# Experts with 33 to 96 tokens past their first 128: three groups behind the tile, groups by column halves, branches ahead of the last tile

## The chip, the cores and the metric

The kernel runs on one core of one Trainium2 chip. The metric is the device time of one execution in microseconds (us). All arithmetic is fp32. The engines are named as in the profile: PE is TensorE (PEld its weight loads), DVE VectorE, ACT ScalarE, POOL GpSimd, SP SyncE; a trailing q means an engine's instruction sequencer (branches, waits on semaphores, issue of DMAs).

## What is computed

A perceiver layer on 512 tokens (8 x 64) of width 512: cross-attention to a context of 1601 rows, a causal linear-attention block with its MLP, and a mixture of experts. Only the last part is touched by the change:

```
logits = x @ w_router                       # 8 experts
top 2 experts per token, softmax over the two logits -> gating
for each expert e:
    hmid = silu(x @ w0[e]) * (x @ w1[e])    # width 1024
    out += gating[:, e] * (hmid @ wo[e])
```

Each expert is needed only for the tokens that chose it. With the inputs of the reference the eight experts have 133, 104, 217, 159, 87, 132, 70 and 122 tokens (counted by running the reference's router). So experts 0, 3 and 5 have 5, 31 and 4 tokens past their first 128, and expert 2 has 89.

## The kernel before, in words

The first stages end at about 424 us. From there the experts run one after the other; everything below is about them.

Order. The program order of every engine is the order of the source (a manual schedule), so what stands behind a wait on an engine waits too. Weights come through a ring of 12 buffers of 1 MB: `need` (L201) frees buffers whose work is past and issues the loads up to 7 places ahead on SP, which in practice loads expert e+1 while expert e is computed. An expert has four `e_up` parts (256 columns of w0 beside 256 of w1, 512 in all) and two `e_wo` parts.

Places. A rank per token and expert gives a table with the tokens of each expert in tiles of 128 (`tabulate`, L924; `late_places`, L1161). `fetch` (L1030) gathers the rows of a tile by an indirect DMA on POOL; `turn_tile` (L1045) transposes them on PE. Tile (e, 0) is the first 128 tokens of expert e; key (e, 1) is the tokens that follow. Unused places point to spare rows.

A whole tile (`whole_tile`, L1088) is, for four quarters of the hidden width: `up` (4 matmuls of 512 columns), silu on ACT and product on DVE (`gated`, L1058), two transposes (`hidden_t`, L1065), and two matmuls into the sum `y`. `add_rows` (L1073) scales by the gate on ACT and adds to the output by an indirect scatter on POOL; each scatter waits for the one before it. Hooks `between(0..2)` put other work into a tile, such as the transposes of the next one.

A group (`group`, L1127) serves up to 32 tokens past the first 128. PE is split into four sets of 32 columns; the four quarters of the hidden width run side by side, one on each: 16 up matmuls of 512 columns, one `gated`, two transposes, 8 down matmuls, a copy of the partial sums (`parts`) and one matmul with `fold` that adds the four. Each step waits for the step before.

Control. The counts are on the chip only. `few` (L1172) is 1 for an expert with 129 to 160 tokens; each engine loads it into registers and branches at the end of each expert (L1326). An `If` that isn't taken runs a short false path instead: each engine waits until its own work so far is done, and adds to its semaphore what the body would have added; POOL runs an INC_SWDGE_SEM there.

Tokens beyond (an expert with over 160, and any third or fourth tile) are handled behind the last expert: `list_big` (L1187) lists such tiles in the order of experts, `big_tile` (L1272) loads the expert's six weight parts again, transposes, and runs `whole_tile`. `all_big` (L1329) nests seven such tiles, each inside the branch of the one before. Here expert 2's 89 tokens are the only such tile.

Of the kernel before, what the change touches and what calls it, by code (L numbers as in the profile page):

```python
# [15 lines left out]
F32 = mybir.dt.float32  # L16
# [17 lines left out]
NQ = 4  # L34
FQ = FE // NQ
R = P // NQ
NI = B * S // P
COLS = 4 * KC + FF // P + KC * NE
HELD = 8
# [7 lines left out]
def perceiver_kernel(  # L47
# [960 lines left out]
    if True:  # L1008


        def side_bank(side, name):
            return pse.tile([P, 512], F32, tag=f"mm{side}", bufs=3 - side, name=name)
# [32 lines left out]
        def turn_tile(key, n=P):  # L1045

            xg = fetched[key]
            name = f"xgt_{key[0]}_{key[1]}"
            bank = (y_bank("w", name) if n == P else side_bank(1, name))
            for c in range(KC):  # L1050
                nc.tensor.transpose(  # L1051
                    bank[:, c * n : (c + 1) * n], xg[:n, c * P : (c + 1) * P], ident[:n, :n]
                )
            xg_t = moe2.tile([P, KC, n], F32, tag=f"xgT{n}", name=f"xgT_{key[0]}_{key[1]}")
            evacuate(xg_t.rearrange("p c q -> p (c q)"), bank[:, : KC * n])
            turned[key] = xg_t

        def gated(side, bank, name):  # L1058
            act = moe2.tile([P, FQ], F32, tag=f"act{side}", name=f"act_{name}")
            nc.scalar.activation(act, bank[:, :FQ], AF.Silu)  # L1060
            hid = moe2.tile([P, FQ], F32, tag=f"mid{side}", name=f"mid_{name}")
            nc.vector.tensor_tensor(hid, bank[:, FQ:], act, ALU.mult)  # L1062
            return hid
# [63 lines left out]
        def group(e, up_of, down_of):  # L1127


            nm = f"{e}_1"  # L1130
            xg_t = turned[e, 1]
            bank = side_bank(1, f"up_{nm}")
            for c in range(KC):
                for q in range(NQ):
                    nc.tensor.matmul(  # L1135
                        bank[q * R : (q + 1) * R, :],
                        xg_t[:, c, :],
                        up_of[q][:, c, :],
                        start=(c == 0),
                        stop=(c == KC - 1),  # L1140
                    )
            h_t = hidden_t(1, gated(1, bank, nm), nm)
            bank = side_bank(1, f"yq_{nm}")
            for j in range(2):
                for q in range(NQ):
                    nc.tensor.matmul(
                        bank[q * R : (q + 1) * R, :],
                        h_t[:, j, q * R : (q + 1) * R],
                        down_of[q // 2][:, 2 * (q % 2) + j, :],
                        start=(j == 0),  # L1150
                        stop=(j == 1),
                    )
            parts = moe2.tile([P, D], F32, tag="parts", bufs=1, name=f"parts_{nm}")
            evacuate(parts, bank)
            y = y_bank(1, f"y_{nm}")
            nc.tensor.matmul(y[:R, :], fold, parts, start=True, stop=True)
            add_rows((e, 1), y, R, 1)

        if True:

# [5 lines left out]
                        slots[e, i] = (src[:, k : k + 1], dst[:, k : k + 1])  # L1166


            few = moe.tile([P, NE], F32, name="few")
            more = moe.tile([P, NE, NI - 1], F32, name="more")  # L1170
            nc.vector.tensor_scalar(more[:, :, 0], count, float(P + R), None, ALU.is_gt)
            nc.vector.scalar_tensor_tensor(few, count, float(P), more[:, :, 0], ALU.is_gt, ALU.subtract)  # L1172
            few_i = moe.tile([1, NE], mybir.dt.int32, name="few_i")
            nc.vector.tensor_copy(few_i, few[0:1, :])
            counted = "sums of comparisons of the experts' counts of tokens"

            def load_few():
                _, values = nc.values_load_multi_w_load_instructions(
                    few_i, min_val=0, max_val=1, skip_runtime_bounds_check_because=counted
                )  # L1180
                return values

            nmore = NE * (NI - 1)
            flat = "p e i -> p (e i)"
            control = moe.tile([1, 1 + 2 * NBIG], mybir.dt.int32, name="control")

            def list_big(k):  # L1187

                if k == 0:
# [9 lines left out]
                        sums, step = new, 2 * step  # L1199
                    listed["sums"] = sums  # L1200
                    nc.vector.tensor_copy(control[:, 0:1], sums[0:1, nmore - 1 :])
                else:
                    by_big = [P, NBIG, nmore]
                    picked = moe.tile(by_big, F32, name="picked")
# [10 lines left out]
                    for v, values in enumerate([number, which_e]):  # L1215
# [4 lines left out]
                        nc.vector.tensor_reduce(  # L1220
                            numbers[:, v * NBIG : (v + 1) * NBIG], found, AX.X, ALU.add
                        )
                    nc.vector.tensor_copy(control[:, 1:], numbers[0:1, :])
                    listed["big_e"] = numbers[:, NBIG:]

            def load_big():
                sp = (mybir.EngineType.SP,)
                _, (big,) = nc.values_load_multi_w_load_instructions(
                    control[:, 0:1], min_val=0, max_val=NBIG, skip_runtime_bounds_check_because=counted
                )  # L1230
                _, spots = nc.values_load_multi_w_load_instructions(
                    control[:, 1 : 1 + NBIG],
                    engines=sp,
                    min_val=0,
                    max_val=NE * NI - 1,
                    skip_runtime_bounds_check_because=counted,
                )
                _, experts = nc.values_load_multi_w_load_instructions(
                    control[:, 1 + NBIG :],
                    engines=sp,  # L1240
                    min_val=0,
                    max_val=NE - 1,
                    skip_runtime_bounds_check_because=counted,
                )
                return big, spots, experts

            listed = {}

# [9 lines left out]
            def gate_big(j):  # L1258
# [10 lines left out]
                )  # L1269
                slots["big", j] += (gate,)  # L1270

            def big_tile(j):  # L1272

                key = ("big", j)
                tiles = {}
                e = bass.ds(listed["experts"][j], 1)
                for q in range(NQ):
                    tiles["up", q] = ring.tile([P, 4, 512], F32, tag="ring", name=f"big_up_{j}_{q}")
                    nc.sync.dma_start(tiles["up", q], e_up[e, q].rearrange("o p c n -> p (o c) n"))
                    if q % 2:  # L1280
                        n = q // 2
                        tiles["wo", n] = ring.tile([P, 4, 512], F32, tag="ring", name=f"big_wo_{j}_{n}")
                        nc.sync.dma_start(
                            tiles["wo", n],
                            e_wo[e, n].rearrange("o p c n -> p (o c) n"),
                        )

                if j > 0:
                    fetch_big(j, read_big(j))
                turn_tile(key)  # L1290
                gate_big(j)
                whole_tile(
                    key,
                    [tiles["up", q] for q in range(NQ)],
                    [tiles["wo", n] for n in range(2)],
                )

            turned[0, 0] = xg_t0
            for e in range(NE):

                def between(k, e=e):
                    if e == 0 and k == 0:
                        late_places()
                        for key in [(1, 0), (0, 1), (0, 0), (1, 1), (2, 0), (2, 1)]:
                            fetch(key, R if key[1] else P)
                    if k == (2 if e == 0 else 1) and e + 1 < NE:
                        turn_tile((e + 1, 0))
                    if k == 2:
                        turn_tile((e, 1), R)
                    if e == 1 and k < 2:  # L1310
                        list_big(k)

                up_of = [need("e_up", e, q) for q in range(NQ)]
                down_of = [need("e_wo", e, n) for n in range(2)]
                whole_tile((e, 0), up_of, down_of, between)
                if e == 0:
                    few_of = load_few()
                if 3 <= e + 2 < NE:
                    for i in range(2):
                        fetch((e + 2, i), R if i else P)  # L1320
                if e == 3:
                    listed["big"], listed["spots"], listed["experts"] = load_big()
                    listed["pairs"] = read_big(0)
                if e == NE - 3:
                    fetch_big(0, listed["pairs"])
                with tc.If(few_of[e] > 0):  # L1326
                    group(e, up_of, down_of)

            def all_big(j):  # L1329
                with tc.If(listed["big"] > j):  # L1330
                    big_tile(j)
                    if j + 1 < NBIG:
                        all_big(j + 1)

            all_big(0)


_INS = [
# [89 lines left out]
```

## Time and profile before

| | us |
|---|---|
| three runs | 673.49, 671.36, 673.45 |
| median | 673.45 |
| the profiled execution | 672.11 |
| its span (first to last instruction) | 670.4 |
| first matmul of expert 0 | at 423.95 |
| tile of expert 1, first up to next tile's first up | 457.39 to 480.43 |
| last matmul of expert 7's tile, ends | at 635.65 |
| last matmul of the tile at the end, ends | at 659.04 |

The span and the profiled time differ by 1.7 us, which lies around the instructions. In the profile a row of a timeline has the start, the length, the engine, the source line, the tiles written and read with their shapes, the number of records, and in brackets how long the engine was idle before and what ended that. A fp32 matmul leaves two MATMUL records on PE and two LDWEIGHTS records on PEld. A row of a table by stretch has the stretch, its length, and for each engine the busy time and number of records, then the granted PE clock (1.00 is full), the DMA share and GB/s. A row by line has the number of records and minimum, median and maximum in ns, then the first and last start in us.

### The profile page before, as it was taken

How to read it: one execution, taken by the hardware profiler on the slowest of the kernel's cores; microseconds unless marked ns; L12 is line 12 of the kernel's file. 1: busy time of each engine (PE TensorE's matmuls, PEld its weight loads, DVE VectorE, ACT ScalarE, POOL GpSimd, SP SyncE). 2: the span in 40 equal slices, each digit the busy share in tenths (PEclk: the TensorE clock that was granted, in tenths of full speed). 3: DMA queues.
4: the chain of work that ended last, by engine and by line, in shares of the span. 5: the costliest groups of instructions: out<-in, count | busy, mean ns of one | idle time of the engine just before them, and what ended most of it. 6: DMA issues, size and time to landing. Idle time of an engine off the chain costs nothing. (4 is left out here: it accounts for less than half of the span.)

```text
span 670.4 us, 6808 instructions
## 1 busy us (share of the span) xinstructions
PE 627.2 (94%) x2664; PEld 291.2 (43%) x2664; DVE 175.5 (26%) x419; ACT 128.3 (19%) x240; POOL 61.6 (9%) x81
## 2 busy tenths in 40 slices
PE   4998989799999999999999998899999899999993
PEld 3743434243444444454444455433444344334441
DVE  4011323122316888650000045311210111100100
ACT  2241222220132223031011211211111211111110
POOL 2000000000000000060000001340202202210000
PEclk9998999899999999999999999799999999999997
DMA  8999999999421203030213115029389576694611
GB/s 326 420 420 389 420 384 418 374 386 413 194 111 43 85 1 127 1 126 18 107 64 125 63 64 188 3 69 350 137 314 337 176 314 229 205 359 177 269 16 19
DMA packets 24224, 138.08 MB, mean 206 GB/s; under 512 B 4164, under 2 KB 4164, under 8 KB 11896
## 3 DMA queue, kind: packets, MB, share of 16 engines
q1 hardware_dynamic: 20056, 129.90, 49.7%
q0 software_dynamic: 3024, 6.58, 4.4%
q10 hardware_dynamic: 1104, 1.07, 0.5%
q8 instruction: 25, 0.41, 0.2%
q14 instruction: 15, 0.12, 0.1%
HBM read 132.56 MB, written 4.97 MB: 205 GB/s over the span
## 5 line engine op out<-in xcount | busy, mean ns | idle before, releaser
L1097 PE MATMUL up<-e_up,xgT 128*128 128x512 f32 x224 | 100.2, 595 | 1.2 <-PEq L1326 1.2
L1097 PEld LDWEIGHTS up<-e_up,xgT 128*128 128x128 f32 x224 | 40.9, 190 | 50.4 <-issue 50.4
L1105 PE MATMUL y<-e_wo,hidT 128*128 128x512 f32 x128 | 61.0, 599 | 0.0
L808 PE MATMUL mlp<-w,hid_sb 128*128 128x512 f32 x128 | 58.8, 597 | 0.0
L1062 DVE TENSOR_TENSOR mid<-up,act 128x256 f32<-128x256 f32 x35 | 14.9, 425 | 162.4 <-ACT act L1060 162.4
L472 PE MATMUL av<-ctx,eT 128*64 128x512 f32 x192 | 50.2, 636 | 7.3 <-DMA ctx<-in_ctx_dram 6.5
L787 PE MATMUL hid<-v_sb,w 128*128 128x512 f32 (+2 forms) x144 | 56.6, 545 | 0.0
L423 PE MATMUL sc<-ctxT,pw_t 128*64 128x401 f32 (+1 forms) x256 | 48.1, 501 | 0.6 <-DMA ctxT<-in_ctx_T_dram 0.6
L787 PEld LDWEIGHTS hid<-v_sb,w 128*128 128x128 f32 x144 | 26.2, 190 | 29.1 <-issue 27.3
L808 PEld LDWEIGHTS mlp<-w,hid_sb 128*128 128x128 f32 x128 | 23.4, 190 | 24.9 <-issue 24.9
L1060 ACT ACTIVATE act<-up 128x256 f32<-128x256 f32 x35 | 13.4, 384 | 104.5 <-PE up L1097 95.6
L1078 POOL DMA_INDIRECT out_dram<-y_sb,dst_late x11 | 16.8, 1530 | 160.9 <-ACTq L1326 103.7
L423 PEld LDWEIGHTS sc<-ctxT,pw_t 128*64 128x64 f32 x256 | 20.2, 136 | 26.0 <-issue 22.6
L802 POOL TENSOR_TENSOR xin<-xin,b_bc 128x512 f32<-128x512 f32 x4 | 5.1, 1269 | 283.4 <-DVE rstd_h L744 279.1
L1105 PEld LDWEIGHTS y<-e_wo,hidT 128*128 128x128 f32 x128 | 22.4, 190 | 19.5 <-issue 19.1
L472 PEld LDWEIGHTS av<-ctx,eT 128*64 128x64 f32 x192 | 15.2, 143 | 35.8 <-issue 24.3
L706 PE MATMUL wo<-wo,a_t 128*128 128x512 f32 x64 | 29.1, 600 | 0.5 <-DVE a_t L682 0.5
L595 PE MATMUL wk<-h_t,wk 128*128 128x512 f32 x64 | 29.5, 604 | 0.0
L595 PE MATMUL wq<-h_t,wq 128*128 128x512 f32 x64 | 29.4, 602 | 0.0
L532 PE MATMUL v<-wv,h_t 128*128 128x512 f32 x64 | 28.7, 597 | 0.6 <-DVE h_t L519 0.6
L680 DVE RECIPROCAL rden<-rden 128x512 f32<-128x512 f32 x8 | 26.8, 3353 | 0.3
L844 DVE TENSOR_TENSOR xs<-mlp,xs 128x512 f32<-128x512 f32 x4 | 2.8, 691 | 87.3 <-PE mlp L808 87.3
(229 smaller groups left out, 630.0 us busy)
## 6 DMA issues: line engine op xcount, KB each, us to landing
e_up<-in_L_ffn_up_dram SPq DMA_DIRECT2D x32, 1024.0 KB, 7.8
ctx<-in_ctx_dram SPq DMA_DIRECT2D x24, 1024.0 KB, 17.4
ctxT<-in_ctx_T_dram SPq DMA_DIRECT2D x24, 802.0 KB, 15.7
e_wo<-in_L_ffn_wo_dram SPq DMA_DIRECT2D x16, 1024.0 KB, 11.3
w<-in_L_attn_w_dram SPq DMA_DIRECT2D x8, 1024.0 KB, 10.9
ctxT<-in_ctx_T_dram SPq DMA_DIRECT2D x8, 796.0 KB, 16.7
big_up<-in_L_ffn_up_dram SPq DMA_DIRECT2D x4, 1024.0 KB, 7.9
wv<-in_L_attn_wv_dram SPq DMA_DIRECT2D x2, 1024.0 KB, 13.1
```

The lines of the kernel that those rows point to most:

```text
L423: nc.tensor.matmul(sc[h * S : (h + 1) * S, :width], pw_t[:, c, (2 * t + h) * S : (2 * t + h + 1) * S], keys[h][:, c, :], start=(c == 0), s ...
L472: nc.tensor.matmul(av[h * S : (h + 1) * S, :], e_t[:, 4 * g + j, h * S : (h + 1) * S], rows[h][:, j, :], start=(g == 0 and j == 0), stop=F ...
L532: nc.tensor.matmul(bank, h_t[:, c, t * P : (t + 1) * P], wv_n[:, c, :], start=(c == 0), stop=(c == KC - 1))
L595: nc.tensor.matmul(bank, w[:, c, (j % 4) * P : (j % 4 + 1) * P], h_t[:, c, :], start=(c == 0), stop=(c == KC - 1),)
L680: nc.vector.reciprocal(rden, rden)
L706: nc.tensor.matmul(wo_banks[t], a_t[:, j, t * P : (t + 1) * P], wo_r[j // 4][:, j % 4, :], start=(j == 0), stop=(j == nj - 1),)
L787: nc.tensor.matmul(hid_banks[f][:, tokens], w[:, c, (f % 4) * P : (f % 4 + 1) * P], h2_t[:, c, tokens], start=(c == 0), stop=(c == KC - 1),)
L808: nc.tensor.matmul(acc[t], hid[:, t * P : (t + 1) * P], need("w2", f // 4)[:, f % 4, :], start=(f == 0), stop=(f == FF // P - 1),)
L1062: nc.vector.tensor_tensor(hid, bank[:, FQ:], act, ALU.mult)
L1078: nc.gpsimd.indirect_dma_start(out=out, out_offset=bass.IndirectOffsetOnAxis(ap=dst[:n, :], axis=0), in_=y_sb[:n, :], in_offset=None, boun ...
L1097: nc.tensor.matmul(bank, xg_t[:, c, :], up_of[q][:, c, :], start=(c == 0), stop=(c == KC - 1))
L1105: nc.tensor.matmul(y, h_t[:, j, :], w[:, 2 * (q % 2) + j, :], start=(q + j == 0), stop=(q + j == NQ))
```

## The change

Four parts.

1. Experts with 161 to 224 tokens (33 to 96 past the first 128) no longer go to the list of tiles at the end. A new `three_groups` runs right behind the expert's tile, with the weights still in the ring: three groups of 32 tokens, interleaved. `few` is now 1 for these, 2 for up to 32 tokens past; over 224 go to the list as before. The gathers of key (e, 1) fetch 96 rows instead of 32.
2. `group` works by halves: the up product of columns 0 to 127 of each part (and of its w1 half), then 128 to 255; silu, product and transpose per half; down by halves of the output columns, with two sums in two PSUM banks; two copies of parts on two engines; two folds of 256 columns.
3. Each of experts 0 to 5 has two branches at its end, `few == 1` and `few == 2`. Experts 6 and 7 have none behind their tiles: ahead of expert 7's tile stands one branch on "anything left" (`control`'s new last entry), and in it their branches and the tiles of the list. The list's tiles load their weights into expert 6's ring buffers.
4. In `between(0)` of experts 0 to 6, a hint on every engine names the next large branch as likely taken (that is, likely to be jumped over).

```diff
+REST = 3 * R
...
         def group(e, up_of, down_of):
...
+            split = "p (w n) -> p w n"
+            halves = [slice(h * P, (h + 1) * P) for h in range(2)]
+            hid = []
+            for h in range(2):
+                bank = side_bank(1, f"up_{nm}_{h}")
+                for c in range(KC):
+                    for q in range(NQ):
+                        nc.tensor.matmul(
+                            bank[q * R : (q + 1) * R, : 2 * P].rearrange(split, w=2),
+                            xg_t[:, c, :],
+                            up_of[q][:, c, :].rearrange(split, w=2)[:, :, halves[h]],
...
+                nc.scalar.activation(act, bank[:, :P], AF.Silu)
+                hid.append(moe2.tile([P, P], F32, tag="mid1", name=f"mid_{nm}_{h}"))
+                nc.vector.tensor_tensor(hid[h], bank[:, P : 2 * P], act, ALU.mult)
...
+            def turn(j):
+                bank = side_bank(1, f"ht_{nm}_1") if j else y_bank(1, f"ht_{nm}_0")
+                nc.tensor.transpose(bank[:, :P], hid[j], ident)
+                h_t[j] = moe2.tile([P, P], F32, tag="hidT1", name=f"hidT_{nm}_{j}")
+                (nc.scalar.copy if j else nc.vector.tensor_copy)(h_t[j], bank[:, :P])
...
+            def down(j, n):
+                if j == 0:
+                    sums[n] = y_bank(1, f"yq_{nm}_1") if n else side_bank(1, f"yq_{nm}_0")
                 for q in range(NQ):
                     nc.tensor.matmul(
+                        sums[n][q * R : (q + 1) * R, : D // 2],
+                        h_t[j][:, q * R : (q + 1) * R],
+                        down_of[q // 2][:, 2 * (q % 2) + j, n * D // 2 : (n + 1) * D // 2],
...
+            turn(0)
+            down(0, 0)
+            turn(1)
+            down(0, 1)
+            parts = []
+            for n in range(2):
+                down(1, n)
+                parts.append(moe2.tile([P, D // 2], F32, tag="parts", name=f"parts_{nm}_{n}"))
+                (nc.scalar.copy if n else nc.vector.tensor_copy)(parts[n], sums[n][:, : D // 2])
+            y = side_bank(1, f"y_{nm}")
+            for n in range(2):
+                nc.tensor.matmul(
+                    y[:R, n * D // 2 : (n + 1) * D // 2], fold, parts[n], start=True, stop=True
+                )
             add_rows((e, 1), y, R, 1)
+
+        def three_groups(e, up_of, down_of):
...
+            def up(g):
+                bank = side_bank(1, f"up_{nm}_{g}")
+                for c in range(KC):
+                    tokens = turned[e, 1][:, c, :] if g == 0 else xg_t3[:, c, g * R : (g + 1) * R]
+                    for q in range(NQ):
+                        nc.tensor.matmul(
+                            bank[q * R : (q + 1) * R, :],
+                            tokens,
+                            up_of[q][:, c, :],
...
+                hid[g] = gated(1, bank, f"{nm}_{g}")
...
+            up(0)
+            up(1)
+            turn(0)
+            up(2)
+            turn(1)
+            down(0)
+            down(1)
+            turn(2)
+            y = side_bank(1, f"y3_{nm}")
+            folded(0)
+            down(2)
+            folded(1)
+            folded(2)
+            add_rows((e, 1), y, REST, 1)
...
-            nc.vector.tensor_scalar(more[:, :, 0], count, float(P + R), None, ALU.is_gt)
-            nc.vector.scalar_tensor_tensor(few, count, float(P), more[:, :, 0], ALU.is_gt, ALU.subtract)
+            nc.vector.tensor_scalar(more[:, :, 0], count, float(P + REST), None, ALU.is_gt)
+            nc.vector.tensor_scalar(few, count, float(P), 2.0, ALU.is_gt, ALU.mult)
+            over = moe.tile([P, NE], F32, name="over_few")
+            nc.vector.tensor_scalar(over, count, float(P + R), None, ALU.is_gt)
+            nc.vector.tensor_tensor(few, few, over, ALU.subtract)
+            nc.vector.tensor_tensor(few, few, more[:, :, 0], ALU.subtract)
...
+            def few_tokens(e, up_of, down_of):
+                with tc.If(few_of[e] == 1, label=f"three_{e}"):
+                    three_groups(e, up_of, down_of)
+                with tc.If(few_of[e] == 2):
+                    group(e, up_of, down_of)
+
+            def hint_ahead(e):
+
+                with tc.block():
+                    tc.mark_branch_hint_location("last_branches" if e == NE - 2 else f"three_{e}", "LikelyTaken", engines=every)
...
+                    if k == 0 and e < NE - 1:
+                        hint_ahead(e)
...
+                if e == NE - 1:
+
+                    with tc.If(listed["any"] > 0, label="last_branches"):
+                        few_tokens(e - 1, *last_weights)
+                        few_tokens(e, up_of, down_of)
+                        all_big(0)
...
                 whole_tile((e, 0), up_of, down_of, between)
...
-                with tc.If(few_of[e] > 0):
-                    group(e, up_of, down_of)
...
+                if e < NE - 2:
+                    few_tokens(e, up_of, down_of)
```

With these inputs the changed program therefore runs `three_groups` behind expert 2, `group` behind experts 0, 3 and 5, and nothing behind experts 6 and 7 nor from the list.

## The prediction, made before the changed kernel was run

> **What bounds the kernel now.** I read the page first. TensorE (PE) is busy for nearly the whole span, so only what shortens PE's own row, or the tail after PE's last instruction, can move the time.
>
> ```profile
> span 670.4 us, 6808 instructions
> PE 627.2 (94%) x2664; PEld 291.2 (43%) x2664; DVE 175.5 (26%) x419; ACT 128.3 (19%) x240; POOL 61.6 (9%) x81
> ```
>
> Then PE's timeline over the experts. It shows a group behind expert 0's tile (the same picture follows experts 3 and 5), a skipped group behind expert 1, and nothing else between tiles.
>
> ```profile
> 446.21 1.98 PE L1105 MATMUL y<-e_wo,hidT 128*128 128x512 f32 x4
> 448.12 3.64 PE L1135 MATMUL up<-e_up,xgT 128*32 128x512 f32 x32
> 452.75 0.44 PE L1068 MATMUL ht<-ident,mid 128*128 128x128 f32 x2 [0.99 <-DVE mid L1062]
> 453.80 1.92 PE L1146 MATMUL yq<-e_wo,hidT 128*32 128x512 f32 x16 [0.61 <-DVE hidT L299]
> 456.42 1.05 PE L1156 MATMUL y<-parts,fold 128*32 128x512 f32 x2 [0.69 <-ACT parts L301]
> 457.39 7.13 PE L1097 MATMUL up<-e_up,xgT 128*128 128x512 f32 x16
> ...
> 480.43 7.10 PE L1097 MATMUL up<-e_up,xgT 128*128 128x512 f32 x16 [0.30 <-PEq L1326]
> ```
>
> In the group PE waits three times (0.99, 0.61, 0.69), each time for an evacuation of its own last product. Third, busy time by stretch: the three groups, the repeated tile of expert 2 at the end, and the tail from the last scatter on.
>
> ```profile
> 448.12:457.39 9.27, 6.98 (x53) 1.77 (x52) 0.85 (x2) 1.66 (x3) 1.60 (x1) 1.00 0.61 138
> 526.10:535.37 9.27, 6.98 (x54) 1.78 (x53) 0.85 (x2) 1.66 (x3) 3.62 (x3) 1.00 0.62 157
> 581.06:590.33 9.27, 6.98 (x54) 1.77 (x53) 0.85 (x2) 1.66 (x3) 4.64 (x4) 1.00 0.60 148
> 635.65:659.04 23.39, 22.40 (x60) 10.14 (x60) 2.36 (x6) 3.56 (x8) 1.55 (x1) 1.00 0.09 13
> 660.04:670.39 10.35, 0.00 (x0) 0.00 (x0) 0.00 (x0) 0.00 (x0) 1.55 (x1) 0.62 0.19 28
> ```
>
> Last, the branches and the end of the program, by line: PE's skip of a group body (L1326) takes at most 348 ns, its one long jump (L1330, over six nested tiles) 3698 ns, and GpSimd's (POOL's) drain at the end 3500 ns.
>
> ```profile
> L1326 PEldq COMPARE_BRANCH  x11: 70/181/348, 445.2 to 632.2; - x11
> L1330 PEldq COMPARE_BRANCH  x3: 70/188/3698, 635.8 to 660.1; - x3
> L1330 POOLq INC_SWDGE_SEM  x1: 1005/1005/1005, 664.9 to 664.9; - x1
> L1424 POOLq DRAIN  x3: 46/109/3500, 666.1 to 670.1; - x3
> ```
>
> **A: expert 2's 89 tokens past 128.** Before, they are the tile at the end: 23.39 us, gone. Three groups come instead. Pitches from the rows above: eight 4-wide sets of up in 3.43 (the start of one set to the next is 0.43), down 1.72, two transposes 0.22, a fold 0.86 (two records of 0.43); changing between 128- and 32-column work costs 0.09 (447.60, the last y record, to 448.12 is 0.52 where 0.43 is usual). So: transposes of 96 rows 0.44; up 3 x 3.43 = 10.29; turns 0.66; down 3 x 1.72 = 5.16; folds 2.58; eight changes 0.75: 19.9, and 0.1 for the last fold, whose evacuation (0.59 and about 0.3 of hand-over) has a fold of 0.86 over it. **20.0**. Its other evacuations lie under the next group's products; if that cover failed, each would cost what the single group shows, 0.6 to 1.0. Part A: 20.0 - 23.4 = **-3.4**.
> Of the moved work, six weight loads (6 MB) vanish from SP. The loads for expert 4, which wait for expert 2's buffers, come 20 us later; tile 4 starts at least 31 us after that, and a load takes 7.8 to 16.4 us to land, so nothing is late. The scatter moves from the end to mid-kernel: POOL is idle there. The gathers of 96 rows instead of 32 issue in the same 1 us; no PE wait for a gather is listed (gathers land 2.7 to 10.1 us after issue; the tightest, expert 0's own, has 5.9, from 439.81 to its use at 445.7). Three times the rows could make that one late: I take 0, between 0 and 1.
>
> **B: three groups by column halves.** Twice the products at half the width. No row has 256 columns on four column groups. The nearest is the 256-wide product with full weights:
>
> ```profile
> 16.83 10.53 PE L368 MATMUL pw<-h_t,w_sb 128*128 128x256 f32 x48
> ```
>
> That is 0.219 each, half of 0.43. The lower bound is this, the upper bound no gain from the halving (0.43). I take 0.216, because the 32-column weight load lasts 109 ns, inside 216. Counting from the first up: both halves issue until 3.46; the last product ends 3.63; ScalarE's silu (0.27, as the 128x128 copy of 266 ns) 3.75 to 4.03; VectorE's product 4.34; then, behind it in VectorE's order, the copy of the first turned half (0.29) to 4.65; down(0,0) 4.75 to 5.18; turn(1), down(0,1) until 5.93; ScalarE's copy is ready at 5.9, so down(1,0) runs to 6.40, down(1,1) to 6.83; the parts are ready at 7.04 and 7.43; folds 7.10 to 7.96; change of width: **8.1** for 9.27. Removed are the wait for the parts and part of the wait for the turned half; what stays late is VectorE's product, then the copy behind it. Part B: 3 x -1.2 = **-3.6**.
>
> **C: more branches at a tile's end.** A skip holds PE until its own last product is through: next up 0.89 after the last record's start (479.54 to 480.43) where 0.43 is usual, so 0.46. Experts 0, 3 and 5 now skip three_groups before their group: +0.4 each (the change of width lies inside it), 1.2. Experts 1 and 4 skip twice; the second adds a compare (0.18 median), an event (0.05) and a jump: +0.3 each, bounds 0.1 and 0.45; 0.6. Expert 2 skips the short group after its three; expert 6 has one skip as before; expert 7's, inside the 23.39, is gone. Part C: **+1.8**.
> Behind a PE branch are the next tile's weights and products alone. POOL's false paths add an INC_SWDGE_SEM of 0.7 to 1.0 us per skip, ahead of its next scatter some 8 to 23 us later: hidden. The hint and its jump in mid-tile have no row; PE decides branches 2.9 us ahead of its products (477.3 for 480.1), so up to 0.35 each is covered: 0. VectorE's three extra operations for the counts (0.17 each) and three in expert 1's tile lie in idle stretches of 4.0 and 3 us: 0.
> Here the Trainium skill speaks against the change ("Runtime: NRT & Kernel Launch", Instruction fetch mechanics): a taken branch whose target is not in the small window of 256-instruction blocks stalls for the fetch. The rows agree: 0.35 for a group of 27 matmuls (4 records each, 108 instructions), 3.70 for the long one. The body of three_groups has 85 matmuls, 340 instructions, so it is out of a block. By the row of short skips C is +1.8. By the rule, unhelped by hints, each first jump (experts 0, 1, 3, 4, 5, last) would show 3.7 - 2.9 = 0.8 and each second one (1 and 4), taken from a drained PE, 3.7: +12.2 more. The hint stands 10 us ahead of each first jump, longer than 3.7, and the second jump has a body of 208 instructions, under one block: I take +1.8, and keep the +14 as a bound.
>
> **D: the tail.** With no branch behind the last scatter, POOL's wait for its landing and the 1.0 of INC_SWDGE_SEM (661.6 to 665.9 in the trace) no longer stand before the drain. The scatter lands 4.65 after its issue; SP's last checks take 0.7, the closing barrier 0.8: 6.2, if the drain of 3.5, from 1.6 on, lies under the landing. If it can only run after the landing: 4.65 + 3.5 + 0.8 = 8.9. The row decides for the first: the drain ran 1.4 us after everything had landed, so it didn't wait for data. Part D: 6.2 - 10.35 = **-4.1** (bound -1.4).
>
> **Sum.** PE's last product comes at 635.65 + 20.0 - 3.6 + 1.8 = 653.9 instead of 659.04; with the tail -3.4 - 3.6 + 1.8 - 4.1 = **-9.3**. The profiled execution took 672.11 (span 670.4): 662.8. The median 673.45 lies 1.3 above it: 664.1 from there. I predict **663.5**.
>
> **Rivals.** (1) The drain waits for the landing: gain 6.6, about 666.2. For it: no row shows a drain with a scatter under way. (2) Blocks of code arrive late at some branches, because expert 2's hint is wrong (its branch isn't taken) or second jumps cross a block: 2 to 6 us back, 665.5 to 669.5. (3) On the other side: half-width products run no faster than full ones on four column groups. Place: 24 sets per group, price 0.214 each, 5.1 per group, 15.4 in all; net +6.1, about 679. It decides from a set pitch of 0.345 on (0.216 + 9.3/72), and the weight load of 109 ns and the row of L368 speak against it. (4) The routing does not do what the change says: with 89 tokens in 96 places it does, unless counts differ; then the tile at the end stays.
>
> **Chances.** Forecast as summed 52% (661 to 665.3: group between 7.6 and 8.6, skips by their bounds); rival 1 20%; rival 2 15%; rival 3 and full stalls (12.2 more: 676) 7%; a better group or tail than summed 6%. Range 660 to 669: it takes in rivals 1 and 2 and leaves out the slow cases. A measurement of this kernel can tell about 0.3%, 2.0 us. Faster than 671.4: 0.89; within: 0.05; slower than 675.5: 0.06.
>
> **What would show it.** Right: a group's window of 8.1 with a set pitch of 0.216; one window of 20 behind expert 2 and no tile behind expert 7; PE's last product near 654; gaps of 0.5 at single, 0.8 at double skips; the last scatter to the end in 6.2. Wrong: a PE branch of microseconds, pitch near 0.43, or a drain that starts after the landing.

## The result, and the profile after

| | before | after |
|---|---|---|
| median (lowest to highest), us | 673.26 (671.36 to 673.82), 6 runs | 667.55 (666.71 to 668.65), 6 runs |
| ratio, 95% interval | | 0.9919 [0.9903, 0.9935] |
| the profiled execution, and its span | 672.11, 670.4 | 666.71, 665.0 |
| first product of expert 0 | 423.95 | 423.12 |
| last product of all, ends | 659.04 | 656.53 |

The change gains 5.7 us where 9.3 were forecast: faster, inside the forecast's range, but some 60% of the sum. PE is as full as before, in a shorter span:

```profile
span 665.0 us, 7383 instructions
PE 625.3 (94%) x2914; PEld 292.5 (44%) x2914; DVE 177.8 (27%) x430; ACT 129.0 (19%) x245; POOL 61.9 (9%) x81
```

PE's timeline after, in the stretches that were shown of before: the group behind expert 0, then the first product behind the double skip of expert 1 and behind the single skip of expert 2, expert 3's group, the double skip of expert 4, expert 5's group, and tile 7.

```profile
448.40 3.66 PE L1149 MATMUL up<-e_up,xgT 128*32 128x256 f32 x64 [1.12 <-ACTq L1421]
451.99 0.33 PE L1164 MATMUL ht<-ident,mid 128*128 128x128 f32 x1
453.14 0.64 PE L1174 MATMUL yq<-e_wo,hidT 128*32 128x256 f32 x8 [0.83 <-DVE hidT L1166]
...
480.04 7.11 PE L1105 MATMUL up<-e_up,xgT 128*128 128x512 f32 x16 [0.72 <-ACTq L1421]
523.16 7.10 PE L1105 MATMUL up<-e_up,xgT 128*128 128x512 f32 x16 [0.30 <-PEq L1423]
546.89 3.66 PE L1149 MATMUL up<-e_up,xgT 128*32 128x256 f32 x64 [1.00 <-ACTq L1421]
578.80 7.10 PE L1105 MATMUL up<-e_up,xgT 128*128 128x512 f32 x16 [1.00 <-ACTq L1423]
602.34 3.66 PE L1149 MATMUL up<-e_up,xgT 128*32 128x256 f32 x64 [0.82 <-ACTq L1421]
634.81 7.11 PE L1105 MATMUL up<-e_up,xgT 128*128 128x512 f32 x16 [1.29 <-DVEq L1462]
```

Inside the group one wait of 0.83 is left of three. What is new stands ahead of the groups: where before a group followed its tile without a pause, it now waits 0.8 to 1.1 for ACT's sequencer at the branch (L1421), and tile 7 waits 1.29 for DVE's. The stretches of the three groups by halves, of the three groups behind expert 2 (with the skip behind them), and of the tail from the last scatter on:

```profile
448.40:456.57 8.17, 7.23 (x102) 3.34 (x102) 1.21 (x4) 1.19 (x4) 1.48 (x1) 1.00 0.68 168
546.89:555.06 8.17, 7.23 (x103) 3.35 (x103) 1.21 (x4) 1.19 (x4) 3.68 (x3) 1.00 0.71 187
602.34:610.52 8.18, 7.23 (x102) 3.36 (x103) 1.20 (x4) 1.19 (x4) 4.69 (x4) 1.00 0.69 180
502.60:523.16 20.56, 20.17 (x161) 6.05 (x160) 2.92 (x7) 3.86 (x8) 3.66 (x3) 1.00 0.17 37
657.53:664.99 7.46, 0.00 (x0) 0.00 (x0) 0.00 (x0) 0.00 (x0) 1.55 (x1) 0.77 0.27 35
```

And the branches and the end, by line: PE's jumps take at most 0.42 us, ACT's false paths (its EVENT_SEMAPHORE) and DVE's are seen, and POOL's drain is longer than the 3500 ns of before.

```profile
L1421 PEldq COMPARE_BRANCH  x7: 78/344/388, 444.3 to 598.0; - x7
L1421 ACTq EVENT_SEMAPHORE  x5: 17/17/17, 448.3 to 602.3; - x5
...
L1462 DVEq COMPARE_BRANCH  x1: 74/74/74, 631.7 to 631.7; - x1
L1462 DVEq EVENT_SEMAPHORE  x1: 21/21/21, 634.5 to 634.5; - x1
...
L1569 POOLq DRAIN  x3: 46/115/6852, 657.3 to 664.7; - x3
```

### The profile page after: what moved, and what is told of

It reads as the page before. It is cut to its first block, busy times and chain, and to the rows that moved or that the text cites. A ratio compares the mean times of both kernels' runs of the same rounds, so it can differ in the third digit from the quotient of the medians.

```text
span 665.0 us, 7383 instructions
## 1 busy us (share of the span) xinstructions
PE 625.3 (94%) x2914; PEld 292.5 (44%) x2914; DVE 177.8 (27%) x430; ACT 129.0 (19%) x245; POOL 61.9 (9%) x81
## 3 DMA queue, kind: packets, MB, share of 16 engines
HBM read 127.33 MB, written 4.91 MB: 199 GB/s over the span
## 5 line engine op out<-in xcount | busy, mean ns | idle before, releaser
L1086 POOL DMA_INDIRECT out_dram<-y_sb,dst_late x12 | 18.3, 1524 | 181.0 <-ACT y_sb L1085 60.1
```

The lines of the kernel that those rows point to most:

```text
L1086: nc.gpsimd.indirect_dma_start(out=out, out_offset=bass.IndirectOffsetOnAxis(ap=dst[:n, :], axis=0), in_=y_sb[:n, :], in_offset=None, boun ...
```

## The experiments

The theory after the result: parts A and B are as summed, part D is smaller since the drain ends behind the scatter's landing, and part C is mis-sized, since a skip was priced by PE's branch alone while the next product waits for the false paths of ACT and DVE. The rival: PE's own branches and code fetches. Kernels with one letter ran on one chip, beside runs of the kernel before on it. A gap below is the time from the start of the last record of a product ahead of a branch to the start of the next one.

| kernel | chip | median (lowest to highest) | before beside it | ratio, 95% interval |
|---|---|---|---|---|
| no hints | A | 668.92 (668.04 to 669.58) | 673.16 | 0.9943 [0.9931, 0.9954] |
| old group | A | 671.87 (670.34 to 673.44) | 673.16 | 0.9987 [0.9977, 0.9996] |
| branches behind the last tile | A | 669.23 (668.38 to 670.04) | 673.16 | 0.9946 [0.9934, 0.9958] |
| up bank apart | A | 666.72 (666.38 to 667.11) | 673.16 | 0.9910 [0.9897, 0.9923] |
| three groups alone | B | 675.41 (674.73 to 676.24) | 673.19 | 1.0032 [1.0020, 1.0044] |
| group first, three groups in the else part | B | 675.15 (672.25 to 677.11) | 673.19 | 1.0027 [1.0018, 1.0037] |
| hints on PE alone | B | 673.79 (672.36 to 675.69) | 673.19 | 1.0009 [0.9998, 1.0020] |
| last scatter of 16 rows | B | 672.64 (one run) | 673.19 | |
| after, again | C | 668.13 (666.59 to 669.59) | 673.26 | 0.9928 [0.9909, 0.9946] |
| group in the else part | C | 663.94 (663.21 to 664.26) | 673.26 | 0.9862 [0.9845, 0.9879] |
| the same, late hint on the other engines | D | 663.39 (661.83 to 664.90) | 673.51 | 0.9849 [0.9834, 0.9863] |
| the same, no hints | D | 668.59 (666.92 to 670.04) | 673.51 | 0.9934 [0.9920, 0.9947] |

The kernel after stands at 667.55 in its first set and at 668.13 in its second, so medians of different chips are compared to no better than some 0.6.

**Part B undone.**

```diff
         def group(e, up_of, down_of):
...
-            for h in range(2):
-                bank = side_bank(1, f"up_{nm}_{h}")
...
+            bank = side_bank(1, f"up_{nm}")
...
+            h_t = hidden_t(1, gated(1, bank, nm), nm)
```

> The changed kernel with the undivided group of before. Theory: each of the three groups takes 9.27 instead of 8.17 us, +3.3, about 670.9 us. Rival (the halves only move the wait, and PE gets it back at the next tile): near 667.5.

671.87, and windows of 9.32 for each group: undoing B costs some 4, and the window says 3 x 1.15 of it. B holds.

**Part D undone** (the branches' block moved behind tile 7).

```diff
-                if e == NE - 1:
-                    with tc.If(listed["any"] > 0, label="last_branches"):
...
                 whole_tile((e, 0), up_of, down_of, between)
...
+                if e == NE - 1:
+                    with tc.If(listed["any"] > 0, label="last_branches"):
```

> The changed kernel with the block of last branches moved behind expert 7's tile. Theory: the gap ahead of tile 7 (1.9 us between the starts of neighbouring products, 1.0 of it for VectorE's late false path) shrinks to the usual 0.43, -1.5; the tail from the last scatter on goes back from 7.5 to about 10.3, +2.9; net +1.4, about 669.0 us. Rival (the shorter tail doesn't come from where the branches stand): only the gap is saved, about 666.1.

669.23. The gap of 1.89 ahead of tile 7 is gone (0.43), and from the last product's end to the span's end it takes 11.09 (after 8.46, before 11.35), with the drain back at 3.5 us:

```profile
L1569 POOLq DRAIN  x3: 46/109/3498, 663.4 to 667.5; - x3
```

So part 3 of the change gives 2.6 at the end and pays 1.5 ahead of tile 7.

**The first up bank of a group taken apart.** The group's first product goes to a PSUM bank that the skipped body doesn't use, so it needn't wait for ACT's false path.

```diff
-                bank = side_bank(1, f"up_{nm}_{h}")
+                bank = side_bank(1, f"up_{nm}_{h}") if h else y_bank("w", f"up_{nm}_{h}")
```

> The changed kernel, with the first half of a group's up products in the PSUM bank of the transposes of whole tiles, which three_groups doesn't use. Theory (the group's first product waits for ScalarE's false path, since its bank was last read in the skipped body, and that path stands behind the scaling of the tile's output, 0.69 us): the gaps of 1.4 to 1.7 us ahead of the three groups shrink to about 0.9, -0.8 each, -2.4 in all: about 665.1 us. Rival (PE's own branch or code fetch sets these gaps): near 667.5.

666.72; the group's first product now waits for PE's own sequencer only:

```profile
449.10 3.66 PE L1149 MATMUL up<-e_up,xgT 128*32 128x256 f32 x64 [0.42 <-PEq L1421]
```

From the last product before it to this one it is 1.02 at all three groups (after: 1.72, 1.60, 1.41). So ACT's false path was 0.4 to 0.7 of each gap, and 0.5 is the price of PE's own false path, about what was forecast. The gain is 1.7 by the gaps and not the 2.4 expected; the median, not measured side by side, is 0.8 below the first set of the kernel after and 1.4 below the second.

**No hints.**

```diff
-                    if k == 0 and e < NE - 1:
-                        hint_ahead(e)
```

> The changed kernel without its hints ahead of the branches; all else as it is. Theory (the hints do fetch the code of a long jump ahead of time): without them each first jump over three_groups or over the last block takes PE some 3.7 us instead of 0.35, of which about 2.9 lie under queued products: 0.8 more at six places, about 672.4 us. Rival (PE's window holds the target anyway, and the hints do nothing): the jumps stay near 0.35 and the time near 667.5, or a few tenths less for the instructions saved. VectorE's late false path ahead of the last tile (2.8 us after its branch) is there either way.

668.92: neither. Three PE jumps take 3.3 to 3.6 us (at 477.4, 544.9 and 631.6), the others 0.4 at most, and most of each long one lies under products that are still queued (PE branches at 477.4, the last product before it ends at 480.3) and under the wait for ACT: the gaps grow by 0.76 at expert 1 and 0.24 at expert 3. Ahead of tile 7 the gap even shrinks, from 1.89 to 1.42, since here DVE's false path comes 0.57 behind its branch instead of 2.89.

**Three groups alone**, put into the kernel before (old group, branches at the end, no hints).

```diff
+        def three_groups(e, up_of, down_of):
...
-                with tc.If(few_of[e] > 0):
+                with tc.If(few_of[e] == 1):
+                    three_groups(e, up_of, down_of)
+                with tc.If(few_of[e] == 2):
                     group(e, up_of, down_of)
```

> The kernel before with the three groups alone: sets of 33 to 96 tokens run as three groups behind the tile, the single group stays at full width, the branches for the last tokens stay at the end, no hints. Theory (the false paths of skipped bodies are the mis-sized term): A gives -3.4, the tail stays as before (0 within 0.5), the three groups ahead of which a body is skipped lose about 1.1 each (3.3), the double skips behind experts 1 and 4 some 0.4 to 0.7 each (1.0): 673.2 - 3.4 + 4.3 = 674, so no gain at all from this part by itself. Rival (skips cost what was predicted, 1.8): 671.6. Long PE jumps of 3.3 to 3.7 us at some skips may add up to 1.

675.41, 2.2 slower than before: part 1 by itself loses. Its window is as in the kernel after (20.14 in both from its first up product to the next tile's), but the gaps of the six tiles grow by 5.5 together, each against before (experts 0 to 6 but 2: 1.2, 0.8, 1.1, 0.9, 0.9, 0.6). The theory's 674 was still too kind.

**Hints on PE alone.**

```diff
-            every = sorted(ordered | {mybir.EngineType.SP}, key=str)
+            every = [mybir.EngineType.PE]
```

> The kernel after with the branch hints on TensorE alone. Theory (VectorE's false path ahead of the last tile comes 2.9 us behind its branch because of its hint's fetch): the gap ahead of tile 7 falls from 1.89 to about 1.4 as it was without any hints, PE's jumps stay at 0.4 at most as with all hints: 667.0. Rival (the gap was PE's own): 667.6, gap 1.9 as before.

The theory falls. Without a hint DVE's false path came 3.03 behind its branch (640.38 to 643.42), and the gap ahead of tile 7 was 2.03. So the hint isn't what delays DVE.

The DMA records tell what does. Code comes by two queues of kind "instruction": packets of 16 KB on q8 follow PE's branches, packets of 8 KB on q14 those of DVE and ACT. A row has the queue, its packets, MB, and the share of the 16 DMA engines' time. Three stretches: in the kernel after, from DVE's branch ahead of tile 7 to its false path (631.6 to 634.5); in "no hints", the same (633.4 to 634.3), the row of all queues; in the kernel after, from PE's hint in expert 1's tile to the branch that it names (465.0 to 476.4).

```profile
q14 instruction: 1, 0.01, 0.7%
...
DMA packets 0, 0.00 MB, mean 0 GB/s; under 512 B 0, under 2 KB 0, under 8 KB 0
...
q8 instruction: 1, 0.02, 0.5%
```

DVE waits for code: in all nine executions with its false path ahead of tile 7 at 2.85 to 3.03 behind its branch, a q14 packet starts 1.02 to 1.06 behind the branch; in the two with 0.57 ("no hints") and 0.54 (group first) none starts before the false path. PE's hint does fetch: in the kernel after a q8 packet starts 3.7 to 3.9 behind three of them, those at experts 1 and 3 and for the last block, just the jumps that are long in "no hints", where none starts between the places of the hints and the branches. DVE's hint (621.8) is followed by no q14 packet before its branch (631.7).

The total, 673.79, can't be compared with the kernel after: here, with the last scatter cut to 16 rows and with the group first (both below), all on chip B, the groups of experts 3 and 5 took longer. The stretches of the three groups and of the tail in the kernel with 16 rows, whose groups are those of the kernel after:

```profile
449.67:457.84 8.17, 7.23 (x102) 3.35 (x103) 1.20 (x4) 1.19 (x4) 1.48 (x1) 1.00 0.71 169
548.15:558.73 10.58, 8.71 (x103) 3.94 (x103) 1.21 (x4) 1.19 (x4) 3.69 (x3) 0.84 0.73 170
605.94:618.25 12.31, 8.68 (x103) 3.82 (x103) 1.21 (x4) 1.19 (x4) 4.70 (x4) 0.86 0.71 170
665.25:670.92 5.67, 0.00 (x0) 0.00 (x0) 0.00 (x0) 0.00 (x0) 1.31 (x1) 0.72 0.06 6
```

In the second and third, ACT starts on the last up product 1.0 and 2.7 us later than in the kernel after, while the tile's scatter is moving; after the pause the granted clock is 0.5 for a while (0.84 and 0.86 over the rows). The kernel after was run again:

> The kernel after, unchanged, beside the others on one chip. In the runs with the hints changed and with the last scatter cut, the groups of experts 3 and 5 took 10.6 and 11.8 to 12.3 us instead of 8.17, though their code and data are those of the kernel after, where all three take 8.17. If that comes from the chip that those ran on (TensorE's signals come 1.0 and 2.7 us late while the tile's scatter runs, then its clock is halved), the kernel after shows it too when it lands on that chip, 672 to 674, and here otherwise 667.5. If it comes from those edits, it is 667.5 on any chip.

668.13, and 8.17 for each group. Edits that touch neither groups nor their data hardly did it; the half-width groups lost 0.7 to 4.1 us apiece at experts 3 and 5 on chip B, where the full-width ones of "three groups alone" took their 9.3. The kernel after itself wasn't run on chip B, and what delays ACT there stays open; kernels of chip B are read by their gaps and windows only.

**The last scatter cut to 16 rows** (most of expert 7's contributions left out).

```diff
-            add_rows(key, y, P, 0)
+            add_rows(key, y, 16 if key == (NE - 1, 0) else P, 0)
```

> The kernel after with the last scatter (tile 7) cut from 128 rows to 16: the contributions of most of expert 7's tokens are left out of the output. It tells what the closing drain of GpSimd waits for. After: scatter issued 657.53, its descriptor work over 659.08, landing seen by SP about 662.4, drain over at 664.15 (6.85 us long). If the drain ends a fixed time behind the landing (about 1.7): the landing comes some 1 to 2 us earlier and the end with it. If the drain works for a fixed time of 3.5 to 5 us behind the end of the scatter's descriptor work: the descriptor work shortens with the rows (to well under 1.55 us), and the end moves by just that much. If neither moves by more than 0.3: the tail is fixed by other things.

Last row above: from the last scatter to the end 5.67 for 7.46, so 1.79 less, while the scatter's own work on POOL is 0.24 shorter. The last packet ended at 667.74 instead of 662.05, 2.49 behind the scatter's issue instead of 4.52, and the drain over 2.3 behind that (after: 2.1).

```profile
L1569 POOLq DRAIN  x3: 46/115/5059, 665.0 to 670.6; - x3
```

So the drain follows the landing. In the ten executions with 128 rows and no branch behind the last scatter it ends 2.09 to 2.13 behind the last packet, but 4.91 to 5.18 behind the end of the scatter's work on POOL. With 16 rows it ends 3.51 behind that work, as long as a drain takes alone (3.5), so there the drain's own work may have ended last.

**One choice per expert.** First with the group in front:

```diff
-                with tc.If(few_of[e] == 1, label=f"three_{e}"):
-                    three_groups(e, up_of, down_of)
-                with tc.If(few_of[e] == 2):
+                with tc.If(few_of[e] == 2) as short:
                     group(e, up_of, down_of)
+                with short.Else():
+                    with tc.If(few_of[e] == 1, label=f"three_{e}"):
+                        three_groups(e, up_of, down_of)
```

> The kernel after with the two branches of an expert turned into one choice: the single group is asked for first, and the three groups stand in its else part. So experts 0, 3 and 5 run their group without having skipped a body; experts 1 and 4 still skip two. Theory (the group's first product waits for ScalarE's false path of the skipped body): gaps ahead of the groups fall from 1.72, 1.60 and 1.41 to about 0.5, so -1.1 each, -3.3: 667.6 - 3.3 = 664.3. If the price only moves to the join behind the group (the way round the else part, taken by every engine), half of it comes back: 666. Rival (PE's own branch is the price, ScalarE only happens to be late): 667.6, gaps ahead of groups or behind them unchanged in sum.

The gaps ahead of the groups are 0.5 as the theory said, but PE's unhinted jump over the else part took 6.93 us behind expert 5's group (0.35 and 0.33 behind the others), and this is one of the three disturbed kernels: 675.15 says nothing more. Then the other way round, with the group in the else part:

```diff
+                with tc.If(few_of[e] == 1, label=f"three_{e}") as three:
+                    three_groups(e, up_of, down_of)
+                with three.Else():
+                    with tc.If(few_of[e] == 2):
+                        group(e, up_of, down_of)
```

> The kernel after with one choice per expert, the other way round than in the earlier run: the three groups first, the single group in the else part. A group is then reached by the hinted jump over the three groups, without a skipped body's false path before it and with no jump behind it. Theory: gaps ahead of groups 0.5 to 0.6 as there (from 1.72, 1.60, 1.41), no long jump behind a group: 3.3 less than the kernel after on the same chip (664.3 where after takes 667.5). Rival (the price moves to TensorE's fetch of the group's code, since the jump leads into the else part): gaps ahead of groups stay at 1.4 or more, within 0.3% of after.

663.94 beside 668.13 for the kernel after: -4.2, expected -3.3. The groups start without a wait, 0.5 behind their tile as before the change, and expert 1's two skips have become a jump and one false path, as costly as one skip. Beside the kernel after on the same chip, the gaps ahead of the three groups are 3.2 shorter in sum, and those at experts 1, 2 and 4, where a jump takes the place of a false path, by some 0.4 each:

```profile
448.72 3.66 PE L1149 MATMUL up<-e_up,xgT 128*32 128x256 f32 x64
479.92 7.11 PE L1105 MATMUL up<-e_up,xgT 128*128 128x512 f32 x16 [0.30 <-PEq L1424]
545.35 3.66 PE L1149 MATMUL up<-e_up,xgT 128*32 128x256 f32 x64
576.82 7.11 PE L1105 MATMUL up<-e_up,xgT 128*128 128x512 f32 x16 [0.58 <-PEq L1424]
599.47 3.66 PE L1149 MATMUL up<-e_up,xgT 128*32 128x256 f32 x64
631.91 7.11 PE L1105 MATMUL up<-e_up,xgT 128*128 128x512 f32 x16 [1.29 <-DVEq L1463]
```

This settles part C: 3.2 of its 5.3 were the groups' waits behind skipped bodies.

**On top of that: hints.** The one for the branch ahead of the last tile, later on all engines but PE:

```diff
-                        hint_ahead(e)
+                        hint_ahead(e, [mybir.EngineType.PE] if e == NE - 2 else every)
+                    if k == 2 and e == NE - 2:
+                        hint_ahead(e, [i for i in every if i != mybir.EngineType.PE])
```

> The kernel with the group in the else part, and the hint for the branch ahead of the last tile given to the engines other than TensorE two parts of a tile later (TensorE keeps its early one). In that kernel VectorE branches at 628.75, 9.9 us behind its hint, and its false path comes only 2.89 us later; tile 7 starts 1.88 behind the last product before it. Theory (the hint comes so early that what it fetched is gone): VectorE's false path then comes 0.6 us behind its branch and the gap falls to 1.4, where ScalarE's false path is last: 0.5 less than the kernel with the group in the else part, 663.4. Rival (VectorE's hint fetches nothing of use): gap 1.9, 663.9.

No: DVE's false path came 3.02 behind its branch, the gap was 2.02, no q14 packet came between DVE's hint, now 2.3 ahead, and its branch, and 663.39 is the same time within the intervals. And no hint at all (the edit of "no hints"):

> The kernel with the group in the else part, without any branch hint. Theory (hints hide a fetch of 3.3 to 3.7 us, TensorE decides a branch 2.9 us ahead of its products): each jump into a block that isn't there costs 0.4 to 0.8 of visible wait; with six such jumps ahead of products, in up to half of them as in the earlier run without hints, +1 to +3: 665 to 667. Rival (the hints do nothing that counts here): 663.9, gaps as with hints. If all six miss: +4 or more.

668.59, 5.2 more than the kernel with the late hint beside it. Four PE jumps take 3.2 to 3.5 us (at 476.7, 543.6, 575.0 and 628.6), against one of 3.4 in the kernel beside it, at expert 4. The gaps grow by 0.8 at expert 1 (0.89 to 1.69), 1.1 at expert 3's group and 1.4 at tile 7 (2.02 to 3.40), and shrink by 0.3 at expert 4: 2.9. That is about the difference of the two profiled executions from expert 0's first product to the last of all (3.1); the rest of the 5.2 isn't in these two, for the profiled one without hints (666.92) is the fastest of its five. The first row below is put down to ACT's scaling (y_sb), but PE's own jump ends as late (546.90). At tile 7 it is ACT's false path that came last, 2.7 behind its branch instead of 0.7, with a q14 packet in between:

```profile
547.21 3.66 PE L1149 MATMUL up<-e_up,xgT 128*32 128x256 f32 x64 [1.02 <-ACT y_sb L1085]
...
635.11 7.13 PE L1105 MATMUL up<-e_up,xgT 128*128 128x512 f32 x16 [2.81 <-ACTq L1459]
```

## Why the prediction was right, and which step was off

667.55 lies in the stated range of 660 to 669, but outside the 661 to 665.3 that the sum was given, and in the stretch of rival 2 (665.5 to 669.5). Parts A and B were right in mechanism and size; C and D were each too kind, and the width of the range took that in. Of the signs named, the group's window and the one window of 20 came; the gaps, the tail and the place of PE's last product did not.

**A, forecast -3.4, measured -3.3.** The three groups take 20.56 with a skip of 0.46 behind them: 20.1, forecast 20.0.

**B, forecast -3.6, measured -3.3.** The up takes 3.66 for twice the records, so a set's pitch is half of before; the group takes 8.17, forecast 8.1. The halving of the products held; the rival that they run no faster (679) is out.

**C, forecast +1.8, measured +5.3.** This is the term that was mis-sized. The gaps:

| behind expert | before | after | rise | forecast |
|---|---|---|---|---|
| 0 | 0.52 | 1.72 | 1.20 | 0.4 |
| 1 | 0.89 | 1.31 | 0.42 | 0.3 |
| 3 | 0.52 | 1.60 | 1.08 | 0.4 |
| 4 | 0.89 | 1.59 | 0.70 | 0.3 |
| 5 | 0.52 | 1.41 | 0.89 | 0.4 |
| 6 | 0.89 | 1.89 | 1.00 | 0 |

The step that failed is "Experts 0, 3 and 5 now skip three_groups before their group: +0.4 each". It took the price from a skip between tiles, where PE's own false path is last. Ahead of a group it isn't: the group's first bank is one that ACT would have read last in the skipped body, so PE waits for ACT's false path, and that stands in ACT's order behind the scaling of the tile's last sum (0.69 us). The bank apart showed it (1.02 left, so 0.5 for PE's own false path where 0.4 was forecast), and the group in the else part removed the whole (0.5, as before the change). The three groups make 2.0 of the 3.5 that C was short. The second failed step is "expert 6 has one skip as before", 1.0: its block's false path on DVE lies 2.9 us behind DVE's branch, since DVE fetches code there, and nothing hid that. The rest, 0.5, is at the double skips, 0.4 of it at expert 4, where the trace puts the wait down to ACT's false path. The text looked at who is queued behind PE's branch and not at the branches of ACT and DVE.

Of the code fetch: the rule cited before (the Trainium skill, "Runtime: NRT & Kernel Launch", Instruction fetch mechanics) was bounded at +12 if unhinted, and set to nothing with hints. With hints PE's jumps are at most 0.42 in the kernel after, so for PE the choice was right. Without them 3 or 4 jumps are long, not all, and up to 1.1 of one is seen, as the lead of PE's decision and the wait for ACT cover the rest. The rule speaks of each engine, and the runs agree: at the last block DVE's false path came 2.9 to 3.0 us behind its branch and once ACT's 2.7, each with a packet of code in between. The prediction asked it of PE's jumps alone; DVE's hint fetched nothing.

**D, forecast -4.1, measured -2.9.** From the last scatter to the end 7.46 instead of 10.35. Neither pure case: the drain begins under the scatter, as forecast, but its 3.5 us, which were to lie under the landing, became 6.85: it ends 2.1 us behind the last packet. The drain of before, by which the prediction decided, ran with no scatter under way and couldn't tell. Rival 1 (landing, then 3.5) would give 8.9 and is too long.

**Sum.** -3.3 - 3.3 + 5.3 - 2.9 = -4.2; 0.4 less in the tiles around (tile 7 has no turn of 32 rows and no branch behind it, tile 6 has the turn) and 0.8 less ahead of expert 0, which differs from one execution to the next, make the -5.4 of the two spans. Against the forecast: C +3.5, D +1.2, A and B +0.4, these two -1.2: 3.9, and 667.55 lies 4.05 above 663.5. Rival 2's number came true mostly by other means: PE's blocks of code were on time. Late code on DVE is 1.0 of the 3.9; most of the rest is ACT's false paths and the drain.

## What to carry to other kernels

A branch that isn't taken costs what the slowest engine needs to get to it and through its false path, if the next product needs a bank that the skipped body would have used; price it on every engine that the product waits for, not on TensorE alone. Where only one of two bodies can run, put the second into the else part of the first, and the one that is often taken where no false path stands ahead of it: here that was worth 4.2 us, more than either of the two parts that shorten the work. A drain behind a scatter ends behind the landing, so moving work from behind the scatter helps only as far as the landing.

## What the runs showed of the hardware

- TensorE's jump over a large body took 3.2 to 3.6 us at some places (on chip B up to 6.9) and 0.3 to 0.4 at others of the same program. The hint, some 11 us ahead, brought nearly all that it names down to 0.4 (one took 1.36, in "old group"); where the jump is long without it, a packet of code of 16 KB started 3.7 to 3.9 us behind the hint (kernel after). Which jumps are long without it changes with the code around.
- On VectorE the same hint fetched nothing: its false path ahead of the last tile came 2.89 us behind its branch with an early hint, 3.02 with a late one, 3.03 and 2.85 without, each time with a packet of code of 8 KB started 1.0 to 1.1 us behind the branch. In two kernels with other code ahead of it (no hints; the group first) it was 0.57 and 0.54, with no packet in between.
- GpSimd's closing drain took 3.5 us with nothing under way, 6.7 to 7.0 with a scatter of 128 rows in flight and 5.06 with one of 16, ending 2.1 to 2.3 us behind the last packet.
- Expert 0's first products take 0.85 us a record instead of 0.43 as long as the granted clock is 0.5, for 3 to 7 records from one profiled execution to the next. The first half of its tile takes 13.97 to 15.63 from this alone, so parts of a microsecond are read from gaps and windows, not from spans.
